# Moving layer 3's signs and products, a chain's steps and a final check in a four-layer attention kernel

## The chip, the cores and the metric

One core of a Trainium2 chip. The metric is the device time of one execution in microseconds (us), the median of several runs. The engines are written as in the profile: PE is TensorE (matmuls), DVE is VectorE, ACT is ScalarE, POOL is GpSimd, and SP is SyncE, which here mainly issues transfers (DMA). Each engine works through its own queue of instructions, and semaphores tie the queues together. Matmuls write to PSUM banks of 128 x 512 fp32; this kernel has eight of them in its main part.

## What is computed

The input is x, 8 images of 512 channels by 32 x 32 pixels, so 1024 positions each, all fp32. Four layers follow one another:

- Layer 0: 1x1 convolutions to 64 channels, f and g with a batch norm and a ReLU, and h. The matrix z = f^T g of an image is divided by its largest singular value and applied to h, and a convolution brings the result back to 512 channels, plus x.
- Layer 1: group norm, then attention over the 1024 positions with 512 channels, softmax included, and a residual addition.
- Layer 2: attention again, with 128 channels for queries, keys and values, a convolution back to 512, and a residual addition.
- Layer 3: the signs of x plus a bias, a 1x1 convolution with the signs of the weights, an affine step, a residual addition, and a leaky step with a slope for each channel.

## The kernel before

**Early part** (to about 173 us in the profile). All eight images are loaded once for the statistics of layer 0. The weights of layer 1 are multiplied with each other beforehand (queries with keys, values with the output projection). The largest singular value of layer 0 comes from a chain of small matrix products for a pair of images: seven rounds of three products, with traces in between, each result turned (transposed) in DVE before it is used again. The chain of the first pair runs in the early part (`first_chain`). The chains of the other three pairs (`chain`, L1313 to L1415) are a generator called `behind`. One step of it is 64-column products on PE, a copy on ACT or DVE, six small transposes on DVE (L1330, L1335), in every third step a trace (L1354, then L1360 to L1361 and a reciprocal, L1383, in the next step), and at the end a logarithm and an exponential on ACT (L1402, L1405). There are 22 steps to a pair.

**Main part.** The function `fast` takes one image after another (n = 0 to 7, in the order 6, 7, 0, ..., 5) through layers 1 to 3 while it prepares the next image:

- Scores of layer 1 (`scores1`, a generator of 28 steps of four 512-column matmul instructions each; a product of fp32 halves is two instructions). They use seven products in the place of eight for 2x2 blocks (`seven`, L365 to L417). One bank holds a product, is copied to a buffer by ACT (`move`, L372) and is then accumulated further by the third, fifth and last of these steps, so each of those must wait for a copy or an addition. The results go to eight buffers of the pool `epool`, which other parts of the kernel use as well.
- Beside the scores, the rest of layer 3 of the image before (`rest3`), the load of the image after next into the buffers that this frees, and from the ninth step on the entering of the next image (`entering`: layer 0's result and the group norm's statistics).
- The values' projection (`make_v`, 14 steps), the sums of the exponentials (`inverse_sums`), and the values' products (`values1`, 14 steps of eight matmul instructions, L756, with additions on DVE and POOL). After the sixth of these the next image is normalized and its blocks' differences are taken on DVE.
- Layer 2: `project2`, then the scores (`scores2`, L1094, with exponentials at L1101 and sums of them at L1088), with the products for the next image's scores (`make_u2`, L611) interleaved. Then `inverse_sums`: eight small matmul instructions with a matrix of ones (L1116), a reciprocal on DVE, and a trip through DRAM that spreads it over the partitions. `values2` (L1256) forms the values for one half of the positions in one bank, and a multiplication on DVE (L1265) makes `att` of it. `close2` projects this and adds it to x (L876, L878), half by half.
- Layer 3 (`leave`): for a half of the positions four signs on ACT (L887), two products of four fp16 matmul instructions (L899), and for each of them evictions on ACT and DVE in turn (L910, L911, L912, L920, L939, L940, L947) and two stores. The first half runs in its own image, the second one is handed to the next image's scores as `rest3`.
- The last image has its own forms: `inverse_rows` (L1145, no trip through DRAM), `last_half` (L974 and after), and `count_bad`, which checks all reciprocals. Its count (L1068, L1069) is loaded into a register of every engine (`values_load`, L1070) for a branch to a slower, general way, which isn't taken here.

**What sets the order.** A planner orders the instructions of DVE, ACT, POOL and SP when the program is built: what comes earlier in the program goes first, but an operation whose inputs it takes to be there can fill a gap. PE's order is the program's, word for word (`manual_schedule`). So a small generator step such as `chore`, which takes one step of `behind`, puts its products at that place in PE's queue:

```
def chore(now):
    if now:
        next(behind, None)
```

In the first image (n = 0), 23 steps are taken: 10 beside the scores, 4 in the values' projection, 5 in the values' products and 4 in layer 2's scores. These are the 22 of the first of the three chains and the first one of the next chain. Later images take 4, 5 and, beside `project2`, 4 more.

Of the kernel before, what the change touches and what calls it, by code (L numbers as in the profile page):

```python
# [21 lines left out]
NT = N // P  # L22
HF = 512
NH = N // HF
NTH = HF // P
# [62 lines left out]
def kernel(  # L88
# [36 lines left out]
    def bank():  # L125
        return psum["bank"].tile([P, HF], F32, tag="bank", name="bank")
# [9 lines left out]
    def load_x(b, split=False):  # L136
        t = xpool.tile([P, CC, N], F32, tag="x", name="xt")
        src = x[b].rearrange("(cc p) n -> p cc n", p=P)
        for cc in range(CC):
            for ns in [half(h) for h in range(NH)] if split and not cc else [slice(0, N)]:  # L140
                nc.sync.dma_start(out=t[:, cc, ns], in_=src[:, cc, ns])
        return t

    def half(i):
        return bass.ts(i, HF)
# [21 lines left out]
    first = load_x(0, True)  # L167
# [165 lines left out]
    def quarters_of(t, rows, cols):  # L333

        return [t[:, rows[k], cols[m]] for m in range(2) for k in range(2)]
# [171 lines left out]
    def split_h(env, ht):  # L507
        hs = env["big"].tile([P, 3, 2, HF], F32, tag="hs", name="hs")
        b = [ht[:, chunks[k], half(n)] for k in range(2) for n in range(2)]
        return differences_of(b, [hs[:, i] for i in range(3)])  # L510
# [535 lines left out]
    def count_bad(env):  # L1046

        g = 2 * B * 4  # L1050
        fine = env["small"].tile([g, NH, P], F32, tag="half_a", name="fine")
        other = env["small"].tile([g, NH, P], F32, tag="half_b", name="other")
        nbad = late.tile([g, 1], F32, tag="nbad", name="nbad")
        first = nc.vector.tensor_scalar(fine, guard, 1.0 / GUARD, None, ALU.is_gt)
        tc.keep_in_program_order(first)
        tc.keep_in_program_order(nc.vector.tensor_scalar(other, guard, GUARD, None, ALU.is_lt))
        nc.vector.tensor_tensor(fine, fine, other, ALU.mult)
        for h in range(NH):
            one = slice(0, g // 2)
            nc.vector.scalar_tensor_tensor(  # L1060
                other[one, h, :], guard[one, 1 - h, :], RATIO, guard[one, h, :], ALU.mult, ALU.is_gt
            )
            nc.vector.tensor_tensor(fine[one, h, :], fine[one, h, :], other[one, h, :], ALU.mult)
        nc.vector.tensor_reduce(nbad, fine.rearrange("p h n -> p (h n)"), AX.X, ALU.min)
        nc.vector.tensor_scalar(nbad, nbad, -1.0, 1.0, ALU.mult, ALU.add)
        yield
        ps = bank()
        mm(out=ps[0:1, 0:1], lhsT=nbad, rhs=ones2[0:g, 0:1], start=True, stop=True)  # L1068
        nc.vector.tensor_copy(bad, ps[0:1, 0:1])  # L1069
        verdict.append(nc.values_load(bad, min_val=0, max_val=P))  # L1070
        yield

# [96 lines left out]
    rest3 = []  # L1169
    verdict = []  # L1170

    def fast(env, n, hb, ua):


        b = order[n]
        xt = resident.pop(b)
        more = n + 1 < B
        ahead = iter(())
# [4 lines that stand above are left out]

        es = [None] * NT
        for k, _ in enumerate(scores1(env, hb, ua, es)):
            if rest3 and k and k % 2 == 0:
                if next(rest3[0], "end") == "end":
                    rest3.pop()
                    if more and order[n + 1] not in resident:
                        resident[order[n + 1]] = load_x(order[n + 1])  # L1190
            if n == 0 and k == 2:
                weights["o"] = sums_of(quarters_of(wo, chunks, cols2), [so[:, i] for i in range(3)], True)
            if n == 0 and k in (9, 11, 13, 15, 17, 19, 21):
                next(late_u)
            if n == 0 and k == 6:
                tp = quarters_of(sbw["tpg"], chunks, [slice(0, P), slice(P, 2 * P)])
                weights["tp"] = sums_of(tp, [sp[:, i] for i in range(3)], True)
            if k == 8 and more:
                ahead = entering(n + 1)


            if k in (10, 13, 20, 27):
                next(ahead, None)
            chore(n == 0 and k in (1, 4, 7, 9, 11, 15, 17, 19, 23, 25))
        esum = es.pop()
        vt = env["big"].tile([P, NT, C], F32, tag="uv", name="vt")
        for k, _ in enumerate(make_v(hb, vt)):
            if k == 3:
                r = inverse_sums(env, esum, n)
            if k == 5:  # L1210
                next(ahead, None)
            chore(k in (1, 7, 10, 13))
        for _ in ahead:
            pass
        scratch = env["big"].tile([P, 3, N], F32, tag="us", name="scratch")
        got = []
        steps = iter(())
        for k, _ in enumerate(values1(env, xt, vt, es, r, scratch)):
            chore(k in (2, 7, 9, 11, 13))
            if k == 5 and more:  # L1220
                nxt = resident[order[n + 1]]
                hb = split_h(env, normal(env, nxt))
                if "jit" not in env:
                    first_u.close()
                    env["jit"] = main.enter_context(
                        tc.tile_pool(name="jit", bufs=1, side="right", reuse_waits="tile")
                    )
                made_u = [prepare_u(env, hb, i) for i in range(2)]
        signs = None
        if more:  # L1230
            steps = make_u2(env, hb, got, made_u)
        else:
            signs = unpacked(env)

        def fill(k=1):
            for _ in range(k):
                next(steps, None)

        made = []
        for k, _ in enumerate(project2(env, xt, made)):  # L1240
            fill()
            chore(n and k in (2, 5, 8, 12))
        tt, pt, gt = made

        def between(t, h):
            fill()
            chore(n == 0 and h and t in (0, 2, 4, 6))

        es, esum = scores2(env, pt, tt, between)
        banks, r = [None, None], None  # L1250

        def values2(h, ts):
            if banks[h] is None:
                banks[h] = bank()
            for t in ts:
                mm(  # L1256
                    out=banks[h],
                    lhsT=gt[:, t, :],
                    rhs=es[t][:, half(h)],
                    start=t == 0,  # L1260
                    stop=t == NT - 1,
                )
            if t == NT - 1:
                att = env["small"].tile([P, HF], F32, tag="half_b", name="att")
                nc.vector.tensor_tensor(att, banks[h], r[:, h, :], ALU.mult)  # L1265
                return att

        dst = channels(out[b])  # L1270
        values2(0, range(0, 2))
        if more:
            r = inverse_sums(env, esum, B + n)
            ua = got.pop()()
            values2(0, range(2, NTH))
            att = values2(0, range(NTH, NT))
            got[0]()
            values2(1, range(0, NTH))
            close2(xt, att, 0)
            att = values2(1, range(NTH, NT))  # L1280
            for _ in leave(env, xt, dst, [0]):
                pass
            close2(xt, att, 1)
            rest3.append(leave(env, xt, dst, [1], stop=True))
            next(rest3[0])
            for _ in steps:
                pass
        else:


            r = inverse_rows(env, esum, B + n)
            att = values2(0, range(2, NT))
            values2(1, range(0, 2))
            close2(xt, att, 0)
            values2(1, range(2, 6))
            before, after = leave(env, xt, dst, [0], signs), last_half(env, xt, dst, signs)
            count = count_bad(env)
            next(count)
            next(before)
            next(before)  # L1300
            att = values2(1, range(6, NT))
            next(before)
            close2(xt, att, 1)
            for _ in before:
                pass
            next(after)
            next(count)
            for _ in after:
                pass

        return hb, ua if more else None

# [211 lines left out]
    env = {}  # L1524
# [107 lines left out]
    for b in range(B):  # L1632
        xt = load_x(b) if b else first
# [410 lines left out]
    with tc.If(verdict[0] > 0):  # L2044
        with (
# [5 lines left out]
            env = {"big": big, "e": epool, "small": small}  # L2051
# [6 lines left out]
            for b in range(B):  # L2058
                xt = load_x(b)
# [43 lines left out]
```

## Time and profile before

| what | us |
|---|---|
| median of 3 runs | 1871.21 (1870.86 to 1872.03) |
| the profiled execution | 1871.17 |
| its span, first to last instruction | 1869.4 |
| PE busy | 1838.7 |
| DVE busy | 1181.1 |
| ACT busy | 568.2 |
| first image, 173 to 394 us: PE busy | 215.35 of 221 |
| third image, 606 to 817 us: PE busy | 209.60 of 211 |
| last image, 1651 to 1869.4 us: PE busy | 207.14 of 218.4 |

The span is that of the core in the profiled execution. The time that runs are compared by is 1.8 us longer in the same execution. Times within the trace are counted from the start of the span. TensorE's clock was granted at 0.999 of its full speed. A row of the timeline has start, duration, engine, line, operation, what is written and read, the shape, and how often; in brackets the idle time of the engine before it, and who ended it. A row of waits has who waited, for whom, then the total in us, the number of waits and the longest.

### The profile page before, as it was taken

What the parts mean: (1) busy time and instruction counts of PE and PEld (TensorE: products, weight loads), DVE (VectorE), ACT (ScalarE), POOL (GpSimd) and SP (SyncE); (2) the same over time, 40 slices, a digit from 0 to 9 for tenths busy, and PEclk for the clock granted to TensorE, in tenths of its full rate; (3) what the DMA queues carried; (4) which work ended last, traced back from release to release, by engine and by line L of the source; (5) the groups of instructions that cost most, each with busy time, mean ns of one, the idle gap of its engine ahead of it and who ended that gap; (6) DMA issues with size and microseconds to landing.
All of it is one profiled execution on the core that took longest, in us unless ns stands there. A gap on an engine that the chain in (4) does not pass through costs nothing.

```text
span 1869.4 us, 18062 instructions
## 1 busy us (share of the span) xinstructions
PE 1838.7 (98%) x6504; PEld 1001.0 (54%) x6504; DVE 1181.1 (63%) x2191; ACT 568.2 (30%) x1020; POOL 383.5 (21%) x402
## 2 busy tenths in 40 slices
PE   9999999989999999999999999999999999999997
PEld 3365464644646465644646455644646464644653
DVE  3357777477765677667775776467654667365447
ACT  2042220344213521244214522244213521244113
POOL 1003004410224003420224003420234004410011
PEclk9999999999999999999999999999999999999999
DMA  8640100332006200242006210242006200330001
GB/s 286 197 138 28 38 18 1 86 81 89 12 10 129 102 27 1 62 99 85 21 2 136 99 31 1 63 99 80 21 10 129 101 22 1 83 80 23 12 1 47
DMA packets 57532, 119.05 MB, mean 64 GB/s; under 512 B 7200, under 2 KB 17244, under 8 KB 57180
## 3 DMA queue, kind: packets, MB, share of 16 engines
q1 hardware_dynamic: 42844, 91.70, 15.0%
q0 software_dynamic: 13728, 25.70, 8.0%
q8 instruction: 53, 0.87, 0.2%
q10 hardware_dynamic: 864, 0.43, 0.1%
q14 instruction: 43, 0.35, 0.1%
HBM read 68.92 MB, written 23.20 MB: 49 GB/s over the span
## 4 chain that ended last, share of the span: by engine, by line
PE 87%; issue 4%; ACT 4%; DVE 3%; DMA 0%; POOL 0%; DVEq 0%; ACTq 0%; POOLq 0%
PE bank L427 35%; PE bank L756 21%; PE bank L611 8%; PE bank L1094 5%; PE bank L1256 5%; PE bank L1644 4%; PE bank L857 3%; PE bank L876 2%; PE bank L451 1%; ACT sg L887 1%; PE bank L899 1%; ACT both L940 1%; ACT up L939 1%; DVE esum L1088 1%; PE bank L1323 1%
## 5 line engine op out<-in xcount | busy, mean ns | idle before, releaser
L756 PE MATMUL bank<-e,vt 128*128 128x512 f32 x768 | 336.2, 594 | 0.0
L756 PEld LDWEIGHTS bank<-e,vt 128*128 128x128 f32 x768 | 144.3, 190 | 172.3 <-issue 166.7
L427 PE MATMUL bank<-ut,h 128*128 128x512 f32 x384 | 178.9, 597 | 0.0
L249 POOL TENSOR_TENSOR r_r<-r_v,minus_half 128x4 f32<-128x4 f32 (+1 forms) x11 | 11.0, 997 | 773.8 <-DVE r_v L248 768.2
L1094 PE MATMUL bank<-tpg 128*128 128x512 f32 x256 | 126.5, 593 | 0.0
L427 PE MATMUL bank<-us,hs 128*128 128x512 f32 x256 | 117.5, 596 | 7.7 <-ACT e L372 7.7
L427 PEld LDWEIGHTS bank<-ut,h 128*128 128x128 f32 x384 | 71.2, 190 | 92.3 <-issue 88.5
L611 PE MATMUL bank<-jit,fac 128*128 128x256 f32 x392 | 117.3, 381 | 1.6 <-ACT p L628 1.4
L1256 PE MATMUL bank<-e,tpg 128*128 128x512 f32 x256 | 114.7, 595 | 0.0
L1101 ACT ACTIVATE e<-bank 128x512 f32<-128x512 f32 x128 | 76.4, 597 | 98.2 <-PE bank L1094 98.2
L611 PEld LDWEIGHTS bank<-jit,fac 128*128 128x128 f32 x392 | 70.5, 190 | 56.4 <-issue 45.3
L378 DVE TENSOR_TENSOR e<-bank,e 128x512 f32<-128x512 f32 x96 | 66.1, 689 | 51.3 <-PE bank L427 51.2
L587 POOL TENSOR_TENSOR jit<-h 128x256 f32<-128x256 f32 x56 | 49.9, 910 | 200.3 <-PE bank L611 113.4
L427 PE MATMUL bank<-wo,h 128*128 128x256 f32 x384 | 89.9, 384 | 0.0
L427 PEld LDWEIGHTS bank<-us,hs 128*128 128x128 f32 x256 | 47.8, 190 | 69.9 <-issue 54.5
L372 ACT COPY e<-bank 128x512 f32<-128x512 f32 x96 | 54.9, 579 | 94.2 <-PE bank L427 94.2
L1256 PEld LDWEIGHTS bank<-e,tpg 128*128 128x128 f32 x256 | 48.1, 190 | 60.4 <-issue 60.3
L427 PEld LDWEIGHTS bank<-wo,h 128*128 128x128 f32 x384 | 71.4, 190 | 12.6 <-issue 3.8
L378 DVE TENSOR_TENSOR vt<-bank,vt 128x512 f32<-128x512 f32 x48 | 33.2, 691 | 66.4 <-PE bank L427 65.5
L372 ACT COPY vt<-bank 128x512 f32<-128x512 f32 x64 | 37.3, 583 | 121.4 <-PE bank L427 121.3
L887 ACT ACTIVATE sg<-xt,rb 128x512 f16<-128x512 f32 x60 | 41.6, 715 | 103.0 <-DVE xt L878 100.2
L628 ACT COPY ut<-bank 128x256 f32<-128x256 f32 x126 | 46.8, 372 | 80.8 <-PE bank L611 79.5
(407 smaller groups left out, 3325.3 us busy)
## 6 DMA issues: line engine op xcount, KB each, us to landing
xt<-in_x SPq DMA_DIRECT2D x55, 512.0 KB
fac<-fac_dram SPq DMA_DIRECT2D x49, 448.0 KB
out<-both SPq DMA_DIRECT2D x63, 256.0 KB
ut<-ut POOLq DMA_DIRECT2D x28, 512.0 KB, 5.0
ut<-p POOLq DMA_DIRECT2D x42, 256.0 KB, 5.3
rfull<-r_dram SPq DMA_DIRECT2D x15, 512.0 KB
f_dram<-f SPq DMA_DIRECT2D x8, 256.0 KB
fb<-f_dram SPq DMA_DIRECT2D x8, 256.0 KB
```

Source lines behind the costliest of these rows:

```text
L372: nc.scalar.copy(dst, ps)
L378: nc.vector.tensor_tensor(dst, ps, u, ALU.add)
L427: mm(out=ps[:, q * w : (q + 1) * w], lhsT=lt(ka, kb, q, k), rhs=rhs(ka, kb, q, k), start=first and q == 0 and k == 0, stop=last and k == 1 ...
L587: tt(t[:, k], b[:, k, hi], b[:, 0, bass.ts(k, QF)], ALU.subtract)
L611: mm(out=out, lhsT=fac[:, blocks[a], :], rhs=rhs[b], start=first, stop=last, skip_group_check=True,)
L756: mm(out=ps, lhsT=a[:, t, bass.ts(r_, P)], rhs=e[t], start=first and t == 0, stop=last and t == NTH - 1, skip_group_check=True,)
L857: mm(out=ps[:, i, :], lhsT=xt[:, cc, bass.ts(4 * h + i, P)], rhs=sbw["tpg"][:, cc, 2 * P : 3 * P], start=cc == 0, stop=cc == CC - 1,)
L887: nc.scalar.activation(sg[:, cc, :], xt[:, cc, half(h)], AF.Sign, bias=rb3[:, cc : cc + 1])
L1094: mm(out=ps, lhsT=pt[:, 0, bass.ts(t, P)], rhs=tt[:, 0, half(h)], start=True, stop=True,)
L1101: nc.scalar.activation(e[:, half(h)], ps, AF.Exp, scale=float(P) ** -0.5)
L1256: mm(out=banks[h], lhsT=gt[:, t, :], rhs=es[t][:, half(h)], start=t == 0, stop=t == NT - 1,)
L1644: one = mm(out=banks[i][side(h), :], lhsT=w0[i][:, cc, :], rhs=xt[:, cc, half(h)], start=cc == 0, stop=cc == CC - 1,)
```

## The change

There are five parts.

1. The second half of layer 3 (`rest3`): its signs were issued at the end of the image; now they are issued after the second score step of the next image. Its first product moves from behind the third score step to behind the fourth, and its second product from behind the fifth to behind the sixth. The load of the image after next moves from the seventh step to the sixth.
2. The first half of layer 3: its signs and first product are put between the sixth and the seventh of the eight products of `values2` for the second half of the positions. The second product stays behind the eighth.
3. Three products of `values2` instead of two stand ahead of the sums (`inverse_sums`, or `inverse_rows` in the last image).
4. In the first image, the four chain steps in layer 2's scores go: one more is taken in the values' projection and three more in the values' products.
5. `count_bad` yields once more before it loads the verdict, and the load is taken behind the last half instead of ahead of it.

```diff
         nc.vector.tensor_copy(bad, ps[0:1, 0:1])
+        yield
         verdict.append(nc.values_load(bad, min_val=0, max_val=P))
...
-            if rest3 and k and k % 2 == 0:
-                if next(rest3[0], "end") == "end":
+            if rest3 and k in (1, 3, 5):
+                next(rest3[0])
+                if k == 5:
                     rest3.pop()
                     if more and order[n + 1] not in resident:
                         resident[order[n + 1]] = load_x(order[n + 1])
...
-            chore(k in (1, 7, 10, 13))
+            chore(k in (1, 7, 10, 13) or n == 0 and k == 4)
...
-            chore(k in (2, 7, 9, 11, 13))
+            chore(k in (2, 7, 9, 11, 13) or n == 0 and k in (8, 10, 12))
...
             fill()
-            chore(n == 0 and h and t in (0, 2, 4, 6))
...
-        values2(0, range(0, 2))
+        values2(0, range(0, 3))
         if more:
             r = inverse_sums(env, esum, B + n)
             ua = got.pop()()
-            values2(0, range(2, NTH))
+            values2(0, range(3, NTH))
             att = values2(0, range(NTH, NT))
             got[0]()
             values2(1, range(0, NTH))
             close2(xt, att, 0)
-            att = values2(1, range(NTH, NT))
-            for _ in leave(env, xt, dst, [0]):
+            values2(1, range(NTH, NTH + 2))
+            first = leave(env, xt, dst, [0])
+            next(first)
+            att = values2(1, range(NTH + 2, NT))
+            for _ in first:
                 pass
             close2(xt, att, 1)
             rest3.append(leave(env, xt, dst, [1], stop=True))
-            next(rest3[0])
...
-            att = values2(0, range(2, NT))
+            att = values2(0, range(3, NT))
...
             next(count)
             for _ in after:
                 pass
+            next(count)
```

## The prediction

> **What bounds the kernel now.** I read the page first: how busy the engines are (its first part), and the chain that ended last (its fourth).
>
> ```profile
> PE 1838.7 (98%) x6504; PEld 1001.0 (54%) x6504; DVE 1181.1 (63%) x2191; ACT 568.2 (30%) x1020; POOL 383.5 (21%) x402
> ...
> PE 87%; issue 4%; ACT 4%; DVE 3%; DMA 0%; POOL 0%; DVEq 0%; ACTq 0%; POOLq 0%
> ```
>
> PE (TensorE) sets the time. No matmul is removed, so the change can win only idle time of PE: 1869.4 - 1838.7 = 30.7 us, start and end included. The view of waits, for PE alone, says where that is.
>
> ```profile
> PE bank L427 <- ACT e L372: 7.7, 7, 1.2
> PE bank L1116 <- DVE half__3045 L1376: 1.7, 1, 1.7
> PE bank L611 <- ACT p L628: 1.4, 1, 1.4
> PE bank L1116 <- DVE esum L1088: 1.4, 6, 0.2
> PE bank L974 <- DVE bad L1069: 1.3, 1, 1.3
> PE bank L611 <- DVE p L622: 1.2, 1, 1.2
> ```
>
> These six rows are 14.7 us, and the change touches the site of each. The first is at the seven boundaries between images. The next question is what ACT does there; the timeline of PE and of ACT, boundary from the seventh image to the eighth:
>
> ```profile
> 1466.68 1.88 PE L427 MATMUL bank<-us,hs 128*128 128x512 f32 x4
> 1469.63 1.98 PE L427 MATMUL bank<-us,hs 128*128 128x512 f32 x4 [1.07 <-ACT e L372]
> 1471.45 1.11 PE L899 MATMUL bank<-sg,sw 128*128 128x512 f16 x4
> 1472.65 1.98 PE L427 MATMUL bank<-us,h 128*128 128x512 f32 x4
> ```
> ```profile
> 1467.09 0.71 ACT L887 ACTIVATE sg<-xt,rb 128x512 f16<-128x512 f32 x1
> ...
> 1469.02 0.56 ACT L372 COPY e<-bank 128x512 f32<-128x512 f32 x1
> 1469.48 0.82 ACT L940 ACTIVATE both<-both,pb,ct 128x512 f32<-128x512 f32 x1
> 1470.20 1.93 ACT L887 ACTIVATE sg<-xt,rb 128x512 f16<-128x512 f32 x3
> 1472.04 1.04 ACT L372 COPY e<-bank 128x512 f32<-128x512 f32 x2
> ```
>
> Layer 3's signs (L887) and evictions (L939, L940) stand ahead of the scores' copies (L372). The third scores step accumulates into the bank that the first copy empties, so PE stands still. PE starts such an fp32 matmul every 0.43 us and an fp16 one every 0.215 (from starts in the timeline). Four take 1.72 or 0.86, but the starts above are 2.95, 1.82 and 1.20 apart, and the following score step (next start 1474.47) takes 1.82: lost 1.23 + 0.10 + 0.34 + 0.10 = 1.77 us per boundary.
>
> **The Trainium skill.** "PSUM — Partial Sum Buffer", Engine vs sequencer instructions: the queues of ACT, DVE (VectorE) and POOL are strictly first in, first out, and matmuls start in program order. The trace agrees: the two copies of 1472.04 stood behind three signs while PE waited. So the order in each queue decides. "ScalarE: Activation LUTs", What ACT_TABLE_LOAD costs: 1283 ns, plus a drain of some 1380. The trace has the 1.28 us, but the next ACTIVATE starts 0.02 us later, so I count no drain. "Perfetto Trace Analysis", Per-instruction lifecycle: a semaphore wait is outside the profiled window; hence I work with starts.
>
> **The change part by part.** The order of DVE and ACT is a planner's, only PE's is written out; I place each vector operation where its inputs and the work ahead of it allow.
>
> *1. Signs of the second half after the second score step; its products one score step later (L1186, L1285).* Removes up to 7 x 1.77 = 12.4 us. Without four signs (starts 0.61 to 0.62 apart, 2.5 us) and with the first half's evictions begun 1.7 us earlier (part 2), the first copy should end about 0.5 us before the third step wants it. The signs then have until the fourth step is done; the next copy behind them has about as much to spare. The second copy can still fall behind the last evictions: bounds 0 and 0.6 us per boundary, half taken: -2.1. The load of the next image moves past one score step, but it waits for the last reader of the image (L920), which comes no earlier. It was landed by 1492.5, and its first reader starts at 1494.47; a boundary that is 1.3 us shorter leaves it hidden. Without that cover, it would cost what it is late.
>
> *2. First products of the first half in the middle of the values' products (L1280).* Four fp16 matmuls change places with four fp32 ones: nothing on PE itself. But the attention result (L1265) now has one product of 0.86 us as cover instead of two. Before, values end at 1459.80, it runs 1460.00 to 1460.69, close2 starts at 1461.53: 0.84 to spare. New, counted from the end of the first product: values end at 1.72, the result can start at 1.92, PE wants it at 2.58. ACT L910 ends at 0.18 + 0.69, L911 at about 1.41 and L912 at 2.13; if L912 is ahead, the result ends at 2.8: 0.27 late, plus the 0.1 that each restart lost above: -0.37 x 7 = -2.6. Bounds: 0.15 (result first) and 1.7 (behind the two L920, 1.35 more).
>
> *3. Third product before the sums (L1271).* At the sums the starts are 0.82 apart where 0.43 is due: +0.39 for six images. But the reciprocal's way through DRAM starts 0.47 later while PE comes 0.39 earlier. The attention result needs 0.86 + 0.06 to spare and had 0.93, 0.82, 0.90, 0.89, 0.58 and 0.96: -0.5. Last image: +0.39, but 0.41 to spare: -0.5. Sum +1.7.
>
> *4. Four turning steps out of the first image's layer 2 (L1212, L1219, L1247).* There the starts show 1.34 + 0.16 + 1.61 + 0.22 + 1.82 = 5.15 us lost (374.00 to 392.94). The largest part is the last step of the first chain: two table loads that hold up an eviction, and with it PE at 383.74:
>
> ```profile
> 379.92 1.28 ACT L1402 ACT_TABLE_LOAD   x1
> ...
> 381.45 1.28 ACT L1405 ACT_TABLE_LOAD   x1
> ```
>
> All of it goes: +5.15. In the new place, the table loads are hidden by ACT's idle 309.5 to 330, with 0.2 us copies alone. DVE isn't idle. The stretches of layer 1's values before and after the next image's normalization:
>
> ```profile
> 281.00:304.40 23.40, 23.40 (x57) 10.49 (x57) 23.13 (x36) 2.09 (x5) 14.44 (x10) 1.00 0.00 1
> 304.40:330.20 25.80, 25.80 (x69) 11.93 (x68) 15.97 (x39) 1.50 (x4) 6.48 (x5) 1.00 0.00 1
> ```
>
> In the first, the third figure after the matmuls, DVE, is 23.13 of 23.40. In the second 9.8 us are free, and steps 20 to 23, which move in, less step 15, which moves to the projection, want about 7.4 (2.1 + 1.4 + 2.8 + 2.5 - 1.4, from rows of these steps). It fits, but each step now has one group of 3.44 us instead of two until PE wants its result. A step with a total takes 3.57 from its product (315.62 to 319.19, two operations of the values between), just within 3.44 + 0.4; one more operation ahead makes it 0.65 late. The chain's end needs a step's turning (0.2 + 0.2 + 0.2 + 1.4), its diagonals (1.45, 373.10 to 374.53) and two operations of the values (1.35): 4.8 against 3.65, 1.2 late. Together -1.85; bounds 0.3 and 4 (DVE full, layer 2's first projection late too).
>
> *5. Verdict last (L1070, L1307).* PE stood from 1855.98 for the loaded verdict. The fourth sign (1856.52) then rules: the first form ends 1.29 earlier, and L982 can start at 1857.2 instead of 1858.27, since L926 runs to 1857.26. The tail follows it: +1.05; bounds 0 and 1.1. The loads (0.5 us) fall while the last store lands (1865.35 to 1867.70).
>
> Sum: 12.4 - 2.1 - 2.6 + 1.7 + 5.15 - 1.85 + 1.05 = 13.75 us. The profiled execution took 1871.17 (span 1869.4), the median is 1871.21, so 1871.2 - 13.8 = **1857.4**.
>
> **The rivals.** A measurement here tells about 0.2%, 3.7 us, from no change.
> - *Attention result behind L920* (part 2's worse bound): 7 x 1.33 = 9.3 less: 1866.7. For: these operations come first in program order; against: L911 of the second product went ahead of L920 in the trace (1462.65 before 1462.98) when it was ready first.
> - *The wait moves on to the fourth or fifth score step*: 1.2 instead of 0.3 left per boundary: 1863.7. For: ACT is nearly full from 1463.8 to 1473; against: 2.5 us of that now comes later.
> - *The signs get ahead of the copies all the same*, since the planner may fill gaps: 12.4 - 2.1 lost: 1867.7, no change.
> - *Slower: the score tiles' buffers.* Scores, signs and outputs share eight. The scores' first two are now taken before the signs', so the next two (eighth step) may get buffers that the second half's last stores hold. ACT's waits at 1482.96 are for store semaphores. The last of those stores goes at about 1486.5 and lands 2.75 later (as 1864.95 to 1867.70), while the copy must be there by 1484.1: some 5.7 us at each boundary, 39.9 - 13.8 = 26.1 slower: 1897. It decides from 13.8 / 7 = 2.0 us per boundary. Against: three of the eight are then free.
>
> **How the numbers follow.** Likeliest 0.62; attention result 0.13; wait moves on 0.10; signs ahead 0.06; buffers 0.09. The likeliest alone runs from 1852 (better bounds of 1, 2 and 4: 2.1 + 1.5 + 1.5 more) to 1861. With the next two the range is 1852 to 1867, and 15 in 100 are left out. Faster 0.85, within 0.2% 0.06, slower 0.09.
>
> **What would show it.** Right: the row of PE waiting for L372 gone or under 2 us; a new row of PE at L876 waiting for DVE att, about 0.3 us seven times; no wait of L611 in the first image, but one or two of L1323 or L1360 on DVE; L974 starting with its signs, right behind L1068. Wrong: L876 waits of over 1 us, a wait of L427 or L899 at the fourth or fifth step, or ACT's copies waiting for a DMA.

## The result and the profile after

| kernel | median, us | runs | ratio to before, 95% interval |
|---|---|---|---|
| before | 1871.31 | 6 (1870.86 to 1872.03) | |
| after | 1861.60 | 6 (1861.15 to 1862.95) | 0.9949 (0.9936 to 0.9962) |

The change wins 9.7 us where 13.75 were forecast. The first and fourth part of the page of after:

```profile
PE 1840.3 (99%) x6504; PEld 1001.1 (54%) x6504; DVE 1183.0 (64%) x2191; ACT 569.6 (31%) x1020; POOL 382.1 (21%) x402
...
PE 86%; DVE 4%; ACT 4%; issue 4%; DMA 1%; POOL 0%; DVEq 0%; POOLq 0%; ACTq 0%; SPq 0%
```

PE still sets the time, and its busy time is that of before but for 1.6 us; the span went from 1869.4 to 1859.9. So the gain is idle time of PE. The view of waits of after, for PE; the rows for setting up the first image, which before has too, are left out:

```profile
PE bank L427 <- ACT e L372: 1.4, 4, 0.4
...
PE bank L1327 <- DVE gm L1339: 1.1, 2, 0.6
...
PE bank L876 <- DVE att L1266: 0.7, 2, 0.4
PE bank L1364 <- DVE diag L1358: 0.7, 1, 0.7
```

The wait for L372 went from seven times, 7.7 us in all, to four times, 1.4. This view counts idle time from the modelled end of the matmul before, which lies behind the normal start of the next, so it leaves out short stalls; the starts, below, show more of the same wait. The rows of L611 on L628 and L622, of L974 on `bad` and of the sums (L1116) on `esum` and `half` are gone. Of the chain, the row of L1364 is new, and that of L1327 (L1323 before) went from one wait of 0.6 us to two.

Where the span changed, cut at the starts of PE's products:

| stretch | after less before, us | forecast |
|---|---|---|
| start to the first image's values (L756) | +0.30 | 0 |
| its values to its `close2` | -3.53 | -3.3 (part 4) |
| the same in the seven later images | -0.14, -0.13, -0.13, -0.56, -0.20, +0.25, +0.01 | -1.7 in all (part 3) |
| seven boundaries (`close2` to the next image's values) | -0.99, -0.38, -1.00, -0.53, -1.09, -0.46, -0.38 | -1.10 each |
| last `close2` to the end | -0.48 | -1.05 |

A trace is one execution. From the first matmul of L427, at 174 us, PE takes 49.28 us to the 112th of them in every trace of this document, to 0.01 us. But some places vary without an edit: what lies ahead of 174 us by up to 0.4 us, layer 2 of the first image by 0.26, and the way of the sums through DRAM by up to 0.8 (see part 3 below).

The boundaries gave 4.83 us in the place of 7.7; this is most of what is missing. The timeline of PE of after, boundary from the second image to the third (the one in the prediction is that from the sixth to the seventh; by the starts, each lost about 1.78 us in before, but the fourth 1.94):

```profile
627.18 1.88 PE L427 MATMUL bank<-us,h 128*128 128x512 f32 x4
628.89 1.11 PE L899 MATMUL bank<-sg,sw 128*128 128x512 f16 x4
630.09 3.70 PE L427 MATMUL bank<-ut,h 128*128 128x512 f32 x8
...
641.36 1.88 PE L427 MATMUL bank<-us,h 128*128 128x512 f32 x4
643.59 3.70 PE L427 MATMUL bank<-ut,h 128*128 128x512 f32 x8 [0.35 <-ACT e L372]
```

And ACT's in the same stretch:

```profile
624.05 0.57 ACT L372 COPY e<-bank 128x512 f32<-128x512 f32 x1
...
627.02 2.55 ACT L887 ACTIVATE sg<-xt,rb 128x512 f16<-128x512 f32 x4
629.47 0.57 ACT L372 COPY e<-bank 128x512 f32<-128x512 f32 x1
...
640.33 1.33 ACT L939 ACTIVATE up<-both,cb 128x512 f32<-128x512 f32 x2
641.57 1.50 ACT L940 ACTIVATE both<-both,pb,ct 128x512 f32<-128x512 f32 x2
642.98 0.56 ACT L372 COPY e<-bank 128x512 f32<-128x512 f32 x1
```

The first copy is in time now: it ends at 624.62, and the third scores step wants it at 625.46. But the third copy stands behind all four signs. It ends at 630.04, and the fifth step starts at 630.09 where 628.89 + 0.86 = 629.75 was due. With the 0.10 us that PE loses when it starts again, that is 0.44 us, at each boundary. A second loss is at the twelfth step, 643.59 where 641.36 + 1.72 = 643.08 was due: its copy stands behind four evictions of the signs' second product. It occurs in four images (0.61 us with the restart). In the other three, four products of `weights0` (L318, for the entering of the next two images) stand at this place and cover it.

The timeline of DVE at the same image's end, and PE's `close2`, which needs `att`:

```profile
616.68 0.43 DVE L911 TENSOR_SCALAR both<-both 128x512 f32<-128x512 f32 x1 [2.61 <-ACT both L910]
617.15 0.69 DVE L912 SCALAR_TENSOR_TENSOR both<-both,bank 128x512 f32<-128x512 f32 x1
617.75 0.69 DVE L1266 TENSOR_TENSOR att<-bank,rfull 128x512 f32<-128x512 f32 x1
618.35 1.41 DVE L920 SCALAR_TENSOR_TENSOR both<-both,sa,xt 128x512 f32<-128x512 f32 x2
```
```profile
617.48 1.03 PE L899 MATMUL bank<-sg,sw 128*128 128x512 f16 x4
618.49 3.70 PE L876 MATMUL bank<-att,z 128*128 128x512 f32 x8
```

L912 is ahead of `att`, L920 behind it, as forecast. `close2` starts at 618.49 in the place of 617.48 + 0.86 = 618.34.

### The profile page after: what moved, and what is told of

It is laid out like the page before. It is cut to its first block, busy times and chain, and to the rows that moved or that the text cites. A ratio compares the mean times of both kernels' runs of the same rounds, so it can differ in the third digit from the quotient of the medians.

```text
span 1859.9 us, 18071 instructions
## 1 busy us (share of the span) xinstructions
PE 1840.3 (99%) x6504; PEld 1001.1 (54%) x6504; DVE 1183.0 (64%) x2191; ACT 569.6 (31%) x1020; POOL 382.1 (21%) x402
## 4 chain that ended last, share of the span: by engine, by line
PE 86%; DVE 4%; ACT 4%; issue 4%; DMA 1%; POOL 0%; DVEq 0%; POOLq 0%; ACTq 0%; SPq 0%
PE bank L427 34%; PE bank L756 20%; PE bank L611 8%; PE bank L1095 6%; PE bank L1257 5%; PE bank L1648 4%; PE bank L857 3%; PE bank L876 2%; PE bank L451 1%; ACT sg L887 1%; PE bank L899 1%; ACT both L940 1%; DVE both L920 1%; ACT up L939 1%; ACT e L372 1%
## 5 line engine op out<-in xcount | busy, mean ns | idle before, releaser
L756 PE MATMUL bank<-e,vt 128*128 128x512 f32 x768 | 336.9, 594 | 0.0
L756 PEld LDWEIGHTS bank<-e,vt 128*128 128x128 f32 x768 | 144.1, 190 | 170.9 <-issue 165.7
L427 PE MATMUL bank<-ut,h 128*128 128x512 f32 x384 | 178.9, 600 | 2.1 <-ACT e L372 1.4
L427 PEld LDWEIGHTS bank<-ut,h 128*128 128x128 f32 x384 | 70.3, 190 | 98.8 <-issue 82.6
L611 PE MATMUL bank<-jit,fac 128*128 128x256 f32 x392 | 117.1, 380 | 0.1
L427 PE MATMUL bank<-us,hs 128*128 128x512 f32 x256 | 115.6, 593 | 0.0
L611 PEld LDWEIGHTS bank<-jit,fac 128*128 128x128 f32 x392 | 70.6, 190 | 54.1 <-issue 45.3
L427 PE MATMUL bank<-wo,h 128*128 128x256 f32 x384 | 90.1, 384 | 0.0
L372 ACT COPY e<-bank 128x512 f32<-128x512 f32 x96 | 55.7, 581 | 102.2 <-PE bank L427 102.1
L427 PEld LDWEIGHTS bank<-us,hs 128*128 128x128 f32 x256 | 48.4, 190 | 59.8 <-issue 59.6
L427 PEld LDWEIGHTS bank<-wo,h 128*128 128x128 f32 x384 | 71.3, 190 | 12.6 <-issue 3.8
L372 ACT COPY vt<-bank 128x512 f32<-128x512 f32 x64 | 37.4, 584 | 117.5 <-PE bank L427 117.4
L628 ACT COPY ut<-bank 128x256 f32<-128x256 f32 x126 | 46.9, 372 | 80.7 <-PE bank L611 79.4
```

The lines of the kernel that those rows point to most:

```text
L372: nc.scalar.copy(dst, ps)
L427: mm(out=ps[:, q * w : (q + 1) * w], lhsT=lt(ka, kb, q, k), rhs=rhs(ka, kb, q, k), start=first and q == 0 and k == 0, stop=last and k == 1 ...
L611: mm(out=out, lhsT=fac[:, blocks[a], :], rhs=rhs[b], start=first, stop=last, skip_group_check=True,)
L756: mm(out=ps, lhsT=a[:, t, bass.ts(r_, P)], rhs=e[t], start=first and t == 0, stop=last and t == NTH - 1, skip_group_check=True,)
```

## The experiments

The stretches are those of the table above, always against before. The kernel before was run on the same chip each time; its medians lie between 1871.0 and 1871.3. An interval of a ratio is 0.07 to 0.17% wide to either side, 1.3 to 3.2 us. Differences of single us between kernels are therefore read from the stretches of the traces, not from the medians.

### Parts 1 and 2 alone

```diff
-            if rest3 and k and k % 2 == 0:
+            if rest3 and k in (1, 3, 5):
...
+            values2(1, range(NTH, NTH + 2))
+            first = leave(env, xt, dst, [0])
+            next(first)
...
-            next(rest3[0])
```

> Parts 1 and 2 alone (layer 3's signs and products moved, everything else as before). Theory: the parts add up, and the seven boundaries are worth what the changed kernel's trace shows between the first L876 of an image and the next image's first L756, 4.8 us in all (7 times 1.77 removed; back come 0.25 for the attention result, 0.44 at the fifth score step for a copy behind the signs, and in four images 0.61 at the twelfth step): 1866.5. Rival, the forecast's own sizes: 12.4 - 2.1 - 2.6 = 7.7 us, 1863.6; then the missing time would lie in how the parts meet.

Measured: 1866.02 us, ratio 0.9972 (0.9962 to 0.9983), boundaries 5.08 shorter. The boundaries give 5 us by themselves; they are not held back by anything that the other parts do.

### Part 4 alone

```diff
-            chore(k in (1, 7, 10, 13))
+            chore(k in (1, 7, 10, 13) or n == 0 and k == 4)
...
-            chore(n == 0 and h and t in (0, 2, 4, 6))
```

> Part 4 alone (the four turning steps out of the first image's layer 2). Theory: 5.15 us of lost starts in layer 2 go, except some 0.4 at the sums, which the third product takes in the whole change; 1.85 come back in layer 1: 3.0 us, 1868.3, with waits of PE at L1323 and L1360 for DVE of 0.6 to 0.7 us. Rival: without the third product the sums still stand behind DVE's work and no more than 2 us are won: 1869.3.

Measured: 1867.82 us, ratio 0.9982 (0.9975 to 0.9989). The stretch from the first image's values to its `close2` is 3.57 shorter, the stretch ahead of its values 0.35 longer; 0.09 of this lies ahead of 174 us, where nothing was edited.

### Part 3 alone

```diff
-        values2(0, range(0, 2))
+        values2(0, range(0, 3))
```

> Part 3 alone (three products ahead of the sums). Theory: in images two to seven the trip through DRAM takes back what the wait for esum gave, 0.9 us left of 2.3; in the first image up to 0.4 more; none in the last: 1.1 us, 1870.2. Rival, the forecast's size: 1.7 us or more, 1869.5, with no wait of L876 for att.

Measured: 1870.25 us, ratio 0.9996 (0.9987 to 1.0005); from values to `close2` 1.96 shorter in all, boundaries 0.58 longer. The runs alone don't tell this from no change, but the forecast +1.7 is too much by the trace: 1.1 from the start to the end, and about half of that comes from the first image, which the forecast didn't count.

### Part 5 alone

```diff
         nc.vector.tensor_copy(bad, ps[0:1, 0:1])
+        yield
...
+            next(count)
```

> Part 5 alone (verdict loaded last). Theory: the last half starts 1.25 us earlier on PE and its additions on DVE 1.0 us earlier; the end follows by 1.05, 1870.2, if the 1.2 us that one store's issue took on SP in the changed kernel's profile is an accident of that execution. Rival: the issue is that slow each time, since the loads lie differently: 0.5 us, 1870.7.

Measured: 1870.5 us, ratio 0.9996 (0.9988 to 1.0005); tail 0.60 shorter, not 1.05; by size this is the rival's 0.5, though one store's issue took 0.76 us here and not 1.2.

The four gains are 5.05 + 3.25 + 0.82 + 0.57 = 9.7, as much as the whole change. Within the width of the intervals the parts add up, so each can be looked at by itself. (The spans of the four traces add up to 10.6 us against 9.5; 0.8 of this is the 0.26 us in the first image's layer 2, which all three kernels that keep the chain as it was have less than before.)

### The second product one step earlier

From here on, the edits are made to the kernel after.

```diff
-            if rest3 and k in (1, 3, 5):
+            if rest3 and k in (1, 3, 4):
                 next(rest3[0])
-                if k == 5:
+                if k == 4:
```

> The changed kernel, but the second half's second product behind the fifth score step instead of the sixth (the load moves with it). Theory: the 0.61 us at the twelfth score step in four images come from that product's late evictions on ACT, ahead of the third copy of the second group; with the product 1.72 us earlier they go: 2.4 us off, 1859.2, and the wait of L427 for L372 there is gone while that of the fifth step stays. Rival: two products so close together crowd ACT and DVE just as much, and the wait stays or turns up at an earlier step: 1861.6 or more.

Measured: 1861.16 us, ratio 0.9948 (0.9931 to 0.9964); the wait at the twelfth step is that of the kernel after (642.63 due, 643.14 started). The theory fell, and the rival held. In this trace everything at this boundary comes 0.45 us earlier than in that of after. PE did the product 2.17 us earlier (631.46 for 633.63), but its first eviction came 0.45 earlier, which is not earlier at all. ACT's timeline of this kernel:

```profile
633.35 1.32 ACT L939 ACTIVATE up<-both,cb 128x512 f32<-128x512 f32 x2
634.58 1.50 ACT L940 ACTIVATE both<-both,pb,ct 128x512 f32<-128x512 f32 x2
635.99 0.66 ACT L910 ACTIVATE both<-bank,round 128x512 f32<-128x512 f32 x1
```

The eviction L910 of the second product stands behind the four of the first. ACT's own order, not the place of the product on PE, decides when its evictions end.

### Signs after the third step

```diff
-            if rest3 and k in (1, 3, 5):
+            if rest3 and k in (2, 4, 5):
```

> The changed kernel, but the second half's signs issued behind the third score step, its first product behind the fifth and its second behind the sixth. Theory: the 0.44 us at the fifth step are the copy that stands behind four signs; issued behind that copy, the signs let it go first, and that wait goes in all seven images: 3.1 us less; the evictions of the first product come 1.72 us later and may add to the wait at the twelfth step, at most as much again: 1858.5 to 1861.6. Rival: the planner puts the signs into ACT's gaps anyway, ahead of the copy: no change, 1861.6.

Measured: 1856.08 us, ratio 0.9919 (0.9902 to 0.9935), an interval that just does not touch that of after; all four executions are at least 4.7 us below all six of after. Boundaries are 10.13 shorter than before, and no wait of L427 for L372 is left. The timeline of PE and of ACT of this kernel:

```profile
626.27 1.88 PE L427 MATMUL bank<-us,h 128*128 128x512 f32 x4
627.99 1.88 PE L427 MATMUL bank<-ut,h 128*128 128x512 f32 x4
...
640.02 1.88 PE L427 MATMUL bank<-us,h 128*128 128x512 f32 x4
641.74 3.66 PE L427 MATMUL bank<-ut,h 128*128 128x512 f32 x8
```
```profile
626.12 0.72 ACT L887 ACTIVATE sg<-xt,rb 128x512 f16<-128x512 f32 x1
626.74 0.57 ACT L372 COPY e<-bank 128x512 f32<-128x512 f32 x1
627.20 1.95 ACT L887 ACTIVATE sg<-xt,rb 128x512 f16<-128x512 f32 x3
...
640.46 0.71 ACT L939 ACTIVATE up<-both,cb 128x512 f32<-128x512 f32 x1
641.08 0.57 ACT L372 COPY e<-bank 128x512 f32<-128x512 f32 x1
641.54 0.82 ACT L940 ACTIVATE both<-both,pb,ct 128x512 f32<-128x512 f32 x1
```

The fifth and the twelfth step start when they are due (1.72 us after the step before). The copy now goes after one sign instead of four. The wait at the twelfth step is gone too: there the copy stands between two evictions, not behind all of them. The same signs and evictions run, in a different order on ACT. The first product also stands one step later on PE, but that alone gives the third copy less time and not more: the fifth step now wants it 0.85 us sooner, counted from the first step. That the copies' place in ACT's order was the cause is shown by this run.

### Without part 2

```diff
-            values2(1, range(NTH, NTH + 2))
-            first = leave(env, xt, dst, [0])
-            next(first)
-            att = values2(1, range(NTH + 2, NT))
-            for _ in first:
+            att = values2(1, range(NTH, NT))
+            for _ in leave(env, xt, dst, [0]):
```

> The changed kernel without part 2 (both products of the first half behind all of the values' products, as before). Theory: the attention result has two products as cover again, so 0.25 us at L876 go seven times (1.75 us), but the first half's evictions begin 1.7 us later on ACT and the first two copies of the scores fall behind them: 0.5 to 1.2 us come back at the third and fourth step, seven times: 1863.4 to 1868.3. Rival: ACT has room without the signs, and part 2 is a loss by itself: 1859.9.

Measured: 1860.76 us, ratio 0.9945 (0.9928 to 0.9961); boundaries 5.48 shorter than before, 0.65 more than with part 2. Without it the second half's `att` is in time (0.25 per boundary won), but the fifth step loses 0.46 + 0.10 instead of 0.34 + 0.10. The loss that the theory expected at the third and fourth step didn't come. In both kernels ACT works without a pause through evictions, signs and the third copy, so half of what PE gains ahead of it is given back there.

### Signs after the third step, without part 2

The edits of the last two, together.

> The kernel of e6 without part 2 (both products of the first half behind all of the values' products). Theory, from e7, where part 2 alone cost 0.65 us: the wait for the attention result goes (0.25 us seven times), and ACT, without signs in front of the first three copies, has the room for the later evictions: 1.0 to 1.7 us below e6, 1854.4 to 1855.1. Rival: the evictions, 1.7 us later, are then in front of the first two copies, and part 2 pays where the signs are out of the way: 1856.6 or more.

Measured: 1854.19 us, ratio 0.991 (0.9893 to 0.9926); boundaries 12.16 shorter, 2.03 more than with the signs' new place alone. With ACT's order out of the way, part 2 costs its seven waits for the second half's `att` and their restarts in full (7 x 0.25 = 1.75); the rest is restarts after a late `att` of the first half, of which this trace has fewer.

### The chain spread further

```diff
-            chore(n == 0 and k in (1, 4, 7, 9, 11, 15, 17, 19, 23, 25))
+            chore(n == 0 and k in (1, 4, 7, 9, 11, 13, 15, 17, 19, 23, 25))
...
-            chore(k in (1, 7, 10, 13) or n == 0 and k == 4)
+            chore(k in ((1, 3, 5, 7, 9, 11, 13) if n == 0 else (1, 7, 10, 13)))
...
-            chore(k in (2, 7, 9, 11, 13) or n == 0 and k in (8, 10, 12))
+            chore(k in (2, 7, 9, 11, 13))
```

> The changed kernel, but the four moved turning steps go one to layer 1's scores (behind the fourteenth step) and three to the values' projection (seven steps there, every second one), none more to the values' products than before. Theory: the two waits there (0.67 and 0.85 us over the due starts, and 0.2 of restarts) go, since two groups lie between the steps again: 1.7 us less, 1859.9. Rival: the projection's DVE or the turning itself is then late every 3.4 us in the same way, and the wait only changes its place: 1861.6.

Measured: 1863.4 us (1861.3 to 1865.52), ratio 0.9956 (0.994 to 0.9973). The waits in the values went (their stretch is 6.41 shorter than before), but the stretch ahead of them grew by 7.15. The step added to the scores has only two score steps between it and the next one, whose input then isn't turned in time. PE's timeline and the table by stretches, in which the last figures are clock, DMA share and GB/s:

```profile
232.53 0.66 PE L1327 MATMUL bank<-cur,gm 128*128 128x64 f32 x2 [2.90 <-DVE gm L1339]
```
```profile
228.00:232.50 4.50, 1.64 (x4) 0.38 (x2) 4.38 (x14) 1.13 (x2) 0.00 (x0) 0.94 0.00 0
232.50:239.00 6.50, 6.47 (x10) 3.00 (x11) 3.18 (x10) 0.80 (x2) 0.00 (x0) 0.51 0.00 0
```

DVE is full in the first stretch (4.38 of 4.50), so the turning waits; and after PE's pause of 2.90 us the clock is at half. The trace is of the execution of 1865.12 us, and the four fall in two pairs: 1865.12 and 1865.52 with a mean clock of 0.996 and 0.997, 1861.68 and 1861.3 with 0.999 and 0.998. So the half clock probably came in two executions of four. 6.8 us at half the clock are worth some 3.4, about the distance of the pairs; without it the spreading brings nothing here, as the rival said.

### The chain spread, without the step in the scores

On top of the signs after the third step:

```diff
-            chore(k in (1, 7, 10, 13) or n == 0 and k == 4)
+            chore(k in ((1, 3, 5, 7, 9, 11, 13) if n == 0 else (1, 7, 10, 13)))
...
-            chore(k in (2, 7, 9, 11, 13) or n == 0 and k in (8, 10, 12))
+            chore(k in (2, 7, 9, 11, 13) or n == 0 and k == 6)
```

> The kernel of e6 (signs behind the third score step, products behind the fifth and sixth), and in the first image the turning steps spread anew: ten beside the scores as before, seven in the values' projection (every second step), six in the values' products (behind the 3rd, 7th, 8th, 10th, 12th and 14th). Theory: what e8 lost, it lost at the one step added to the scores (2.9 us of waiting for DVE, then 6.8 us at half the clock); without that one, the waits of 0.67 and 0.85 us in the values' products and their restarts go, and at most 0.4 comes back in the projection: 1.3 us below e6, 1854.8, with TensorE's clock never under full before the end. Rival: a step every 3.4 us in the projection is late too: 1856.1 or more.

Measured: 1853.79 us, ratio 0.9908 (0.9892 to 0.9925); the waits in the values are gone (-6.24 against before, -3.73 without the spreading), 0.76 comes back in the stretch ahead, of which 0.61 lies behind the 174 us, where the edit is. The clock stays at full up to the last 6 us.

### The verdict loaded earlier in the last half

The load, `next(count)`, moves from behind the last half into it:

```diff
         form(3)
+        load()
         scaled(2, zs[:, 0], qb3)
...
-            next(count)
```

> The changed kernel, with the verdict's load issued within the last half, behind its fourth product, instead of behind all of it. Theory: the slow issue of a store on SP (764 ns with the verdict alone, 1217 in the changed kernel, 332 to 362 in the others) comes from the register load that DVE makes at the same time, between its last operations; with DVE's load earlier the stores take 0.33 to 0.4 us each and the end comes 0.5 us earlier: 1861.1. Rival: the two only happen together, and the store is slow again: 1861.6.

Measured: 1861.16 us, ratio 0.9946 (0.993 to 0.9963). The time is the theory's, but one of the last stores still takes 0.97 us to issue, though DVE's load of the verdict is out of its way. The theory that this load holds up the store fell. It rested on a misreading too: the "332 to 362 in the others" are medians, and the kernel with parts 1 and 2 alone, which loads the verdict where it was before, has an issue of 0.93 us.

### All three placements together

Without part 2, signs after the third step, chain spread.

> The whole change with three placements put otherwise: the signs behind the third, fifth and sixth score steps, part 2 left out (the second half's last values in one stretch, its products behind them), and the chain's seven steps spread further over make_v and values1. Theory: the two best single improvements do not touch each other, so their gains add: 1854.2 us of the kernel without part 2 less the 2.3 us that the spread chain was worth beside the signs' new places, so 1851.9 us (1851.3 to 1852.5), with no wait of TensorE for ACT or DVE left at the boundaries between images nor in the values of the first image; boundaries shorter than before by about 12.2 us in all. Rival: the evictions that the chain's steps delay in the first image come back at the first boundary, which no longer has a free pause to take them in: 1853.3 us or more, with a wait over 0.5 us at line 876 or 372 in the first boundary.

Measured: 1852.94 us (1852.73 to 1853.05), ratio 0.9903 (0.9886 to 0.9919), the lowest median of all, but not to be told from 1853.79 by these intervals. The time is between what theory and rival expected. In the traces, the gains do not add in full. Against the kernel without the spreading, the first image's values give 2.37 more, but the later images lose about 1.4 in all. Most of this is the first `close2` of an image, which waits a little for `att`, and the restarts behind it. DVE's timeline of this kernel, second image:

```profile
598.96 1.76 DVE L1126 RECIPROCAL rsum<-bank 128x256 f32<-128x256 f32 x1 [1.32 <-PE bank L1117]
...
606.12 0.69 DVE L1266 TENSOR_TENSOR att<-bank,rfull 128x512 f32<-128x512 f32 x1 [0.79 <-DMA rfull<-r_dram]
```

From the reciprocal's end to `att`, 606.12 - 600.72 = 5.40 us; in the kernel without the spreading it is 5.00 in this image. The trip through DRAM took 0.4 longer, and PE has next to nothing in hand there since part 3. The spreading isn't shown to be the reason: with it the trips take 5.27 to 5.45 us here but 5.00 to 5.23 in the kernel of 1853.79, and without it 4.99 to 5.50 in that of 1854.19 but 5.30 to 5.62 in that of 1860.76. What sets the trip's length stays open. The rival expected a wait of over 0.5 us at the first boundary; the starts there are 0.51 apart where 0.43 is due (396.32 to 396.83), so it is 0.08, and what comes back is spread over the images.

## Why the prediction was right, and where not

The direction, the bound and the parts' rank were right: PE's idle time at the boundaries and in the first image's layer 2 paid, and no rival came true in the size given. But 1861.60 is 4.2 us above the forecast, just outside the 1852 to 1861 that the likeliest course was given alone, and nearer to the rival *the wait moves on* (1863.7). The prediction's signs came out on both sides: the row of L372 is under 2 us, as it should be if right, and there is a wait at the fifth step, as there should be if wrong. The row was too weak a sign. It says 1.4 us, the starts say 5.5, since the view leaves out the fifth step's stall. And by luck two errors of size worked against each other: 3.4 us too little at part 1, 0.85 too much at part 2. By its own terms:

- **12.4 of part 1: right.** The 1.77 us per boundary at the third and following steps went.
- **-2.1 of part 1: the step that failed.** It held that the signs "have until the fourth step is done", with the next copy behind them as much in time, and took 0.3 us of 0 to 0.6 for each boundary. In after it is 7 x 0.44 = 3.1 at the fifth step and 4 x 0.61 = 2.4 at the twelfth, 5.5 us. The signs begin only at 627.02, behind an eviction, and take 2.55 us, while the copy behind them had to start at 629.18 to be in time. The twelfth step was not looked at. The rival *the wait moves on* had the mechanism, but named the fourth or fifth step, and its size of 1.2 per boundary came to 0.79, the twelfth step included. That ACT's order is the cause is shown by moving the signs one step on (-10.13 for -4.83).
- **-2.6 of part 2: order right, size too large.** `att` ran between L912 and L920, and the loss was 0.25 per boundary, 1.75 in all, for 2.6. The bound "behind the two L920" did not occur. Part 2 wins nothing that was seen: 0.65 and 2.03 us of boundaries are to be had by leaving it out.
- **+1.7 of part 3: too much, about 0.5.** At the sums 0.30 was won in an image (starts 0.52 apart in after, 0.82 before), for 0.39. And the sum took each image's way from the reciprocal's end to `att` to be as long as in the trace of before, 5.04 to 5.52 us. In after it takes 5.07 to 5.75, and over all fourteen traces 4.99 to 5.75, with no edit to it. With part 3, `att` is late by what this way exceeds some 5.19 us (5.24 is 0.06 too late, 5.75 is 0.55). In after it is late in five of the first seven images, by 1.11 us in all (the second: 607.77 + 1.72 = 609.49 due, 609.65 started), and each time 0.10 for the restart is lost as well, which the sum left out. The last image is 0.50 late, as forecast.
- **+5.15 - 1.85 of part 4: right.** The waits at layer 2 went. In layer 1's values two new ones came, at the places named; PE's timeline of after:

```profile
324.54 0.43 PE L1327 MATMUL bank<-cur,gm 128*128 128x64 f32 x2 [0.51 <-DVE gm L1339]
...
329.15 0.38 PE L1364 MATMUL bank<-td,mask 128*128 128x2 f32 x2 [0.69 <-DVE diag L1358]
```

  The starts ahead of them are 323.44 and 327.87, so they are 0.67 and 0.85 late (0.65 and 1.2 forecast). With the two restarts and the 0.26 that the step in the values' projection costs, 3.2 us are left of 5.15; 3.3 were forecast.
- **+1.05 of part 5: mechanism right, half of it given back.** L974 starts right behind L1068, and the DVE work of the tail comes 1.0 earlier against `close2`. But issuing the last stores takes longer. SP's transfers of the last line, after and then before (minimum, median and maximum in ns):

```profile
L1010 SPq DMA_DIRECT2D out<-both x5: 332/398/1217, 1852.1 to 1855.3; - x5
```
```profile
L1010 SPq DMA_DIRECT2D out<-both x5: 332/332/402, 1862.0 to 1864.9; - x5
```

  A single issue of 1.22 us, the second of the five, holds up the last three by some 0.3 us. Its cause is open. In the kernel of 1853.79 us, where no issue takes over 0.40, the tail is 0.88 shorter than before.
- **The slower rival, the buffers:** no copy of ACT waited for a transfer in after. Its point of decision was not reached.

## What to carry to other kernels

- When work is moved out of the way of one wait, list every later instruction of the same engine that something waits for, up to the point where the queue has a pause again, and give each its latest start. The copies for the fifth and the twelfth step would have shown in such a list.
- On an engine that another one waits for, the length of a block without a break counts. Four signs in one piece made a copy late; one sign, the copy and three signs did not.
- A gap that has been won is worth little if a queue without a pause lies right behind it: leaving out part 2 brought 0.65 us with the signs in the way and 2.03 without.
- Judge a stall by the starts. The view of waits gave 1.4 us where the starts gave 5.5.
- A transfer that is just covered in one trace may not be in the next: over these traces the trip through DRAM varies by 0.8 us.

## What was not expected of the hardware

- PE's pause of 2.90 us in the main part (3.06 by the starts: 229.04 + 0.43 to 232.53) was followed by 6.8 us at about half the clock (0.51 in the table above), in which 512-column fp32 matmuls started 0.85 us apart instead of 0.43. The waits of PE in the main part of before, up to 1.7 us, left the clock alone. By their mean clocks, two of the kernel's four executions did not fall to half, though how long PE paused in those two isn't on record. The Trainium skill, "TensorE: Matmul & The Clock Gate", Part 1: The HAM clock gate, gives half the clock as what follows an idle window of some 3.4 us, and a busy window of that length to leave it. The trace agrees in kind; the idle time that sufficed here was less, and the half clock lasted about two such windows.
- The slowest of SP's last five store issues took 397 to 425 ns in five of the kernels (before among them), and 558 to 1217 ns in the nine others, by one trace of each. Neither the place of the verdict's load nor the length of the tail goes with it.
- After each of the stalls at the boundaries in before and after, the next 512-column fp32 matmul started 0.53 us later instead of 0.43 (delays of a few hundredths brought less). A wait of PE thus cost 0.1 us more than its length.
